# More places for turned blocks and queries, prepared weights stored by GpSimd, and right operands made early around the outer product with most sums

## The chip, the cores and the metric

The kernel runs on one core of a Trainium2 chip. The time is device microseconds of one execution, and the median of several executions is compared. Profiles show TensorE as PE (its weight loads as PEld), VectorE as DVE, ScalarE as ACT, GpSimd as POOL and the queue of SyncE, which issues most DMAs, as SP.

## The reference

A decoder layer in float32 on x of 16 x 128 x 1024, with three residual steps: self-attention with one head of 256, a linear cross-attention, and a gated feed-forward network whose weights are packed int4 with scale and zero for each group of 64.

```python
x = x + attn(layernorm(x), Wqkv, bqkv, Wo, bo)
x = x + xattn(layernorm(x), ctx, ctx, Wq, Wk, Wv, Wo, bo, g)
x = x + ffn(layernorm(x), gate, up, down)

def xattn(q, k, v, ...):          # channel-first, 8 heads of 64, n = 1024
    qh = softmax(Wq q, over the 64 of a head) * SCALE
    kh = softmax(Wk k, over n)
    context = einsum('bhdn,bhen->bhde', kh, Wv v)
    out = Wo einsum('bhde,bhdn->bhen', context, qh) + bo
    return out / max(norm(out), 1e-12) * g * sqrt(128)

def ffn(x, ...):                  # hidden 1024, inter 2752
    g, u = x @ Wg.T, x @ Wu.T     # Wg, Wu, Wd dequantized from int4
    return (silu(g) * u) @ Wd.T
```

## The kernel before

The order of work on each engine is that in which the Python code emits it; a tile framework adds the waits. Tiles come from pools with a fixed number of places (bufs): a new tile waits until the last reader of the tile that held its place is done. DMAs are issued in order by the queue of the engine that is named (SP, ACT or POOL), and several are in flight at once.

*Self-attention, 0 to 250 us.* Its last products, give_half, are emitted in the next stage: each of 8 calls multiplies half of a batch's attention output by Wo, and VectorE adds it to X and takes the batch's statistics. The two tiles of Wo are loaded again for them (wo_again, in the pool of the queries).

*Linear cross-attention, 250 to 855 us.* It goes over 16 batches (batches 8 to 15, then 0 to 7; k counts them). Each batch has eight ticks of some 3.9 us: key_unit and query_unit in turn, four times. Work is put off with later(n, fn), which runs fn at the n-th next tick. A query unit multiplies (kq) and ScalarE exponentiates (qe). Two ticks later weigh lets VectorE sum (sums) and invert (qrec) and POOL multiply qe. Four ticks later turn lets VectorE transpose 32 x 32 blocks into kt (pool b_kt), which a DMA on SP writes to DRAM as kd; one tick later four DMAs on SP read it as qs (pool b_qs), the turned queries. Keys go through ek, and VectorE sums them into ksum, whose column sums PE needs in mix for the small matrix m_sb of the batch. project_out multiplies qs by m_sb at the ticks in when, takes norms (on PE and ScalarE), and then VectorE scales (y), adds to X (add) and takes statistics; turned normalises the rows and turn_rows transposes them into kt as well, to be stored and loaded as the blocks of the feed-forward network (block_loads, 8 loads of 512 KB for each half of the batches). raise_flag tests all sums for overflow; count multiplies the result by ones on PE and VectorE copies the flag.

*Preparation beside it.* prepare is a generator, one step of which dequantizes half a 256-wide block of a weight matrix (DVE pa<-raw, pa<-pa,sz), or combines its quarters for Strassen's algorithm (pc), and stores all seven operands to DRAM, to wg, wu, wm, wr or wd. It runs in three parts: early (in the self-attention, stores on POOL), middle (in the cross-attention, two or three steps a batch, stores on SP) and rest (the down weights, in the feed-forward stage, stores on SP). prep_pools gives its pools: a places for pa, ahead + 1 for the loaded raw and sz.

*Feed-forward, 855 to 1774 us, and down projection, 1774 to 2254 us.* Two passes over 1024 rows each. Pass 0 takes blocks 0 to 3 with one level of Strassen (one_block; PE p<-b,w), then three pairs of blocks with two levels (two_levels, 1000 to 1274 us), then a last block; pass 1 takes five pairs with two levels. two_levels goes over outer products in the order DOWN = (1, 2, 6, 5, 3, 7, 4) for each pair; each has seven inner products p of eight matmuls (1.72 us). The right operands of outer q that are differences come from inner_right: four VectorE subtractions ti (k = 7, 5, 6, 4; p = 7, 5, 6, 4 read them). The left ones, li, come from POOL. The list right holds the steps for the next outer's ti, extra holds less urgent ones; do_extra(n, more) runs n of the first and more of the second between products. got adds finished products into the sums U, V and C on VectorE: 3 additions where q is 1, 11 where q is 7, and 7 for each other q. Then ScalarE takes SiLU of half of C and VectorE multiplies (h). PSUM is banked in turn between two pools of four.

The names that the change touches: pools b_kt and b_qs (lines 610 and 614), the middle preparation (620), count (691), block_loads (856), the ticks of give_half (941), when (954), prep_pools for the rest (1050), bufs of ti (1328) and the list right in two_levels (1497).

Of the kernel before, what the change touches and what calls it, by code (L numbers as in the profile page):

```python
# [11 lines left out]
F32 = mybir.dt.float32  # L12
# [6 lines left out]
P = 128  # L19
# [47 lines left out]
def decoder_layer(  # L67
# [482 lines left out]
    blocks = {}  # L550
    TOKENS = TB // Q

    def block_loads(p, blocks):

        for n, half in ((0, 0), (1, 0), (1, 1), (0, 1)):
            for i in range(2):
                src = xt_all[p][ds(half * BPT + 2 * i, 2), :, :, :, n]
                tc.keep_in_program_order(
                    nc.sync.dma_start(
                        blocks[n, half][:, ts(i, TOKENS // 2)],  # L560
                        src.rearrange("b a c i j t -> (c i) (b a) j t"),
                    )
                )
                yield
# [42 lines left out]
    b0 = unit_pool("b_0", 2)  # L607
    bw = unit_pool("b_w", 1)
    b3 = unit_pool("b_3", 3)
    bkt = side_pool("b_kt", 2)  # L610
    bpk = unit_pool("b_k", 2, space=PSUM)
    bs = side_pool("b_s", 1)
    bct = side_pool("b_ct", 2)
    bqs = side_pool("b_qs", 4)
    b1 = side_pool("b_1", 1)
    b2 = side_pool("b_2", 2)
    bps = side_pool("b_ps", 3, space=PSUM)

    prep_pools(sides, "x", 2, 1)
    middle = prepare(todo[EARLY:MIDDLE], 1, sync, vector, sync)  # L620


    pend = deque()
# [1 line left out]
    def later(n, fn):  # L625
        pend.append([n, fn])
# [10 lines left out]
    if True:  # L637
# [33 lines left out]
            sums = bs.tile([P, B * 4 * 2 * HEADS + B * 4], F32, name="sums")  # L671

        def sums_tile(n, at, name):
            return sums[:, ds(at, n)] if plain else small.tile([P, n], F32, name=name)

        def raise_flag():

            within = [small.tile([P, 1], F32, name=f"within{n}") for n in range(2)]
            for w, op, limit, test in zip(
                within, (ALU.max, ALU.min), (LIMIT, 1 / LIMIT), (ALU.is_le, ALU.is_ge)  # L680
            ):
                vector.tensor_reduce(w, sums, AX.X, op)
                vector.tensor_scalar(w, w, limit, None, test)
            vector.tensor_tensor(within[0], within[0], within[1], ALU.mult)

            def count():
                ps = bps.tile([P, 1], F32, name="mm")
                tensor.matmul(ps, ones, within[0], start=True, stop=True)
                vector.tensor_copy(flag, ps[0:1])

            later(2, count)

        def mix_weights():

# [14 lines left out]
        def key_shift(c_sb):  # L709

            shift = bas.tile([P, 4, P], F32, name="kshift")
            for oc in range(4):
                ps = bpk.tile([P, 2, 512], F32, name="kq")
                for h in range(2):
                    tensor.matmul(
                        ps[:, h, :], wk_sb[:, ts(oc, P)], c_sb[:, ts(h, 512)], start=True, stop=True
                    )
                nmax = small.tile([P, 1], F32, name="knmax")
                vector.tensor_reduce(nmax, ps, AX.XY, ALU.max, negate=True)
                vector.tensor_copy(shift[:, oc], nmax.to_broadcast([P, P]))  # L720
            return shift
# [45 lines left out]
        def mix(st):  # L767

            D = DIM_HEAD
            ks = bps.tile([P, 4], F32, name="mm")  # L770
            for r in range(4):
                tensor.matmul(
                    ks[:, r : r + 1], st["sum"][:, 0, ts(r, P)], ones[:, 0:1], start=True, stop=True
                )
            ksum = sums_tile(4, B * 8 * HEADS + 4 * st["b"], "ksum")
            krec = small.tile([P, 4], F32, name="krec")
            vector.tensor_copy(ksum, ks)
            vector.reciprocal(krec, ksum)
            kc = st["kc"]
            mp = bps.tile([P, 4, S], F32, name="mm")  # L780
            for r in range(4):

                for e in range(2):
                    tensor.matmul(
                        mp[ts(e, D), r, :],
                        kc[:, ds(r * P + e * D, D)],
                        g_sb[:, 2 * r + e, :],
                        start=True,
                        stop=True,
                    )  # L790
            st["m"] = b2.tile([P, 4, S], F32, name="m_sb")
            vector.tensor_tensor(
                st["m"], mp, krec.unsqueeze(2).to_broadcast([P, 4, S]), ALU.mult
            )

        def query_unit(b, pair, qs, wait):

            wide = [P, 2 * HEADS, DIM_HEAD]
            ps = bpk.tile([P, 2, 512], F32, name="kq")
            for i in range(2):  # L800
                tensor.matmul(
                    ps[:, i, :], xns[b][:, ts(2 * pair + i, P)], wq_sb, start=True, stop=True
                )
            heads = ps.rearrange("p i (h d) -> p (i h) d", d=DIM_HEAD)
            qe = b3.tile(wide, F32, name="qe")
            if plain:
                nc.scalar.activation(qe, heads, AF.Exp)  # L807
            else:
                mx = small.tile([P, 2 * HEADS], F32, name="qmx")
                vector.tensor_reduce(mx, heads, AX.X, ALU.max)  # L810
                vector.tensor_tensor(qe, heads, mx.unsqueeze(2).to_broadcast(wide), ALU.subtract)
                nc.scalar.activation(qe, qe, AF.Exp)

            def weigh():
                den = sums_tile(2 * HEADS, (4 * b + pair) * 2 * HEADS, "qden")
                rec = small.tile([P, 2 * HEADS], F32, name="qrec")
                vector.tensor_reduce(den, qe, AX.X, ALU.add)
                vector.reciprocal(rec, den)
                nc.gpsimd.tensor_tensor(qe, qe, rec.unsqueeze(2).to_broadcast(wide), ALU.mult)  # L819

            def turn():
                kt = bkt.tile([P, 4, NB, Q], F32, name="kt")
                vector.transpose(
                    kt.rearrange("p c n j -> p n c j"),
                    qe.rearrange("p h d -> p (h d)").rearrange("p (n c j) -> p n c j", c=4, j=Q),
                )
                kd = dram.tile([4, Q, 4, NB, Q], F32, name="kd", tag="kd", bufs=3)
                sync.dma_start(kd.rearrange("a i c n j -> (a i) c n j"), kt)  # L830

                def load():
                    qt = qs[pair] = bqs.tile([P, 4, NB, Q], F32, name="qs", tag="qs")
                    for c in range(4):
                        sync.dma_start(
                            qt[ts(c, Q)], kd[:, :, c].rearrange("a i n j -> i a n j")
                        )

                later(1, load)

            later(2, weigh)
            later(wait, turn)

        def turned(b):

            xn = b1.tile([P, 2 * JC, P], F32, name="xn3")
            for n in range(2):

                rows = X[b].rearrange("p (g j e n) -> p n j g e", g=16, j=JC, n=2)[:, n]
                dst = xn[:, ts(n, JC)].rearrange("p j (g e) -> p j g e", g=16)  # L850
                normalise_act(dst, rows, b)
            nc.gpsimd.dma_start(x_all[b], X[b])
            later(2, lambda: turn_rows(b, xn, bkt))
            if b == B - 1:
                blocks.update(new_blocks(xlate, lambda k: f"X{HB + 2 * k}"))
                loads = block_loads(0, blocks)
                for n in range(8):
                    later(7 + 2 * n, lambda: next(loads))

# [78 lines left out]

        for n in range(2 * BPT):
            later(  # L940
                n + 1,
                lambda n=n: give_half(B - BPT + n // 2, n % 2, oT, wo_again, bps, tensor, vector),
            )
        keys = {b: {"b": b} for b in batches}
# [3 lines left out]
        for k, b in enumerate(batches):  # L948
# [2 lines left out]


            if len(ahead) == 2:
                when = (13, 14, 15, 16, 17, 1, 1)
            elif ahead:
                when = (12, 13, 14, 15, 16, 1, 0)
            else:
                when = (10, 10, 11, 11, 12, 1, 0)
# [75 lines left out]
    with ExitStack() as gs:  # L1034
# [9 lines left out]
        def attention_done():  # L1044
# [2 lines left out]
            for _ in middle:  # L1047
                pass
            sides.close()
            prep_pools(second, "f", 3, 2)  # L1050
            rest = prepare(todo[MIDDLE:], 2, nc.sync, vector)
            banks.append(pool("c_u", 4, space=PSUM, side="right"))

# [248 lines left out]
        class Operands:  # L1302
# [5 lines left out]
            def inner_right(self, q):  # L1308
# [10 lines left out]
                def comb(k):  # L1319
                    if k == 7:  # L1320
# [4 lines left out]
                            F32,  # L1325
                            name="ti",
                            tag=tag,
                            bufs=1 if self.kept else 2,
                        )
                    dst = R[q, k] = R[q][:, (5, 6, 7, 4).index(k)]  # L1330
                    a, b = {
# [31 lines left out]
        def two_levels(ps, pairs, operands, between=lambda q: None):  # L1363
# [115 lines left out]
            for n, (i, q) in enumerate(OUTERS):  # L1479
# [13 lines left out]
                    soon_due.popleft()()  # L1493
                if q not in (1, 5):
                    sums["C"] = place.tile(wide, F32, name="C")
                if not last:
                    right.extend(operands.inner_right(OUTERS[n + 1][1]))
                if ps == 1 and n == 0:
                    extra.append(lambda: outer_operand(operands.T, 4))
                elif ps == 1 and n == 4:  # L1500
# [403 lines left out]
```

## Time and profile before

| what | us |
|---|---|
| median of 3 runs | 2255.17 (2254.84 to 2259.01) |
| the profiled execution | 2256.0, its span 2254.2 |
| PE busy | 2201.5 (98%) |
| VectorE busy | 1611.7 (71%) |
| ScalarE busy | 512.0 (23%) |
| GpSimd busy | 594.9 (26%) |
| mean granted clock of PE | 0.989 |

Shares of the whole span hide the stages: VectorE is busy for 92 us of every 100 between 300 and 600 us and for 58 to 86 of 100 from 600 to 1300 us. A list of waits is read as: engine, operation and line that waited, what ended the wait, total us, times, longest us. Most lines are 63, a helper that records operations, so groups are told apart by tiles: kt<-qe is the transposition of qe into kt. In a row of the stage table each engine has its busy us and in brackets its instructions, in the order PE, PEld, DVE, ACT, POOL; then follow the granted clock, the DMA share and GB/s.

### The profile page before, as it was taken

To read this page: it belongs to the slowest core of one execution; us is meant where nothing else is said; L and a number is where in the kernel's file an instruction comes from. 1 tells how busy PE (TensorE), PEld (TensorE's weight loads), DVE (VectorE), ACT (ScalarE), POOL (GpSimd) and SP (SyncE) were. 2 spreads that over 40 slices of the span, in tenths; PEclk is the share of its full clock that TensorE was granted. 3 is DMA by queue.
4 is the path that set the end of the run, shared out by engine and by line. 5 is a ranking of instruction groups with operands and counts; after the bars stand their busy time and mean duration, and the time that the engine had idled before them with its cause. 6 is when DMAs were issued, how large, how long until landed. Compare 5 with 4: busy or idle time off the path is not lost.

```text
span 2254.2 us, 24858 instructions
## 1 busy us (share of the span) xinstructions
PE 2201.5 (98%) x8666; PEld 1588.1 (70%) x8666; DVE 1611.7 (71%) x2185; ACT 512.0 (23%) x690; POOL 594.9 (26%) x450
## 2 busy tenths in 40 slices
PE   8999999999989999999999999999999999999998
PEld 7556555555545554458878678888887688888887
DVE  6997589999988656658888768787786545544462
ACT  2111135655545541111112111211211000000000
POOL 5452123333333320014434144444442000000000
PEclk9999999999999999999999999999999999999999
DMA  6445358888888569984333534554554974333731
GB/s 250 156 135 181 112 171 253 261 252 273 247 255 270 187 198 284 313 280 139 130 99 128 168 125 140 178 196 150 178 193 162 336 237 150 125 124 128 225 117 39
DMA packets 270006, 425.28 MB, mean 189 GB/s; under 512 B 28784, under 2 KB 130544, under 8 KB 269744
## 3 DMA queue, kind: packets, MB, share of 16 engines
q1 hardware_dynamic: 242752, 374.31, 52.4%
q0 software_dynamic: 9104, 30.68, 3.7%
q10 hardware_dynamic: 18016, 18.62, 2.6%
q8 instruction: 71, 1.16, 0.2%
q14 instruction: 63, 0.52, 0.1%
HBM read 265.62 MB, written 157.35 MB: 188 GB/s over the span
## 4 chain that ended last, share of the span: by engine, by line
PE 76%; DVE 14%; DMA 3%; issue 3%; POOL 2%; ACT 1%; SPq 0%; DVEq 0%; POOLq 0%; ACTq 0%
PE q L63 26%; PE po L1783 21%; PE p L63 10%; PE kq L63 4%; PE mm L63 4%; PE mm L397 4%; DVE pa L63 3%; PE kx L63 2%; PE mm L412 2%; DVE kt L63 2%; PE p L1160 2%; DVE sums L63 1%; PE mm L295 1%; DVE ti L63 1%; DVE pc L63 1%
## 5 line engine op out<-in xcount | busy, mean ns | idle before, releaser
L63 PE MATMUL q<-ti,li 128*128 128x256 f32 x1344 | 315.4, 384 | 11.0 <-DVE ti L63 10.2
L63 PEld LDWEIGHTS q<-ti,li 128*128 128x128 f32 x1344 | 257.6, 192 | 49.8 <-issue 9.9
L63 POOL TENSOR_TENSOR li<-w 128x512 f32<-128x512 f32 x112 | 159.9, 1429 | 258.2 <-DMA raw<-in_dq 140.6
L63 ACT COPY k<-q 128x512 f32<-128x512 f32 x168 | 98.4, 585 | 540.1 <-PE q L63 540.1
L819 POOL TENSOR_TENSOR qe<-qe,qrec 128x1024 f32<-128x1024 f32 x64 | 145.3, 2270 | 249.8 <-DVE qrec L63 206.3
L1783 PE MATMUL po<-wc,lc 128*128 128x256 f32 x840 | 183.4, 379 | 0.0
L1783 PEld LDWEIGHTS po<-wc,lc 128*128 128x128 f32 x840 | 159.6, 190 | 21.8
L63 PEld LDWEIGHTS mm<-qs,m_sb 128*128 128x128 f32 x512 | 99.0, 194 | 53.2 <-issue 38.0
L63 PE MATMUL mm<-qs,m_sb 128*128 128x256 f32 x512 | 124.9, 388 | 10.9 <-DMA qs<-kd 10.9
L63 PE MATMUL p<-b,w 128*128 128x512 f32 x304 | 133.9, 592 | 0.0
L63 POOL TENSOR_TENSOR li<-w,li 128x512 f32<-128x512 f32 x56 | 75.5, 1347 | 209.3 <-PE q L63 207.1
L1783 PE MATMUL po<-wq,lq 128*128 128x256 f32 x560 | 126.7, 379 | 0.4 <-issue 0.4
L63 PE MATMUL kx<-ek,cxt 128*128 128x512 f32 x256 | 125.6, 614 | 0.3 <-ACT ek L739 0.3
L63 PE MATMUL kq<-wq_sb,xn 128*128 128x512 f32 x256 | 121.7, 598 | 1.6 <-ACT qe L807 1.6
L63 PE MATMUL kq<-wk_sb,cx 128*128 128x512 f32 x256 | 122.0, 599 | 0.0
L63 PE MATMUL q<-b,w 128*128 128x256 f32 x512 | 120.9, 379 | 0.0
L63 DVE TENSOR_TENSOR C<-q,k 128x512 f32<-128x512 f32 x120 | 82.2, 685 | 53.4 <-PE q L63 51.2
L1783 PEld LDWEIGHTS po<-wq,lq 128*128 128x128 f32 x560 | 106.0, 190 | 16.0 <-issue 1.2
L63 DVE STREAM_TRANSPOSE kt<-qe 128x1024 f32<-128x1024 f32 x64 | 79.4, 1240 | 51.1 <-POOL qe L819 41.4
L397 PE MATMUL mm<-xnT,wqkv_sb 128*128 128x512 f32 (+1 forms) x320 | 113.1, 509 | 0.0
L63 DVE TENSOR_TENSOR pa<-pa,sz 128x1024 f32<-128x1024 int32 x86 | 108.8, 1265 | 3.6 <-DMA sz<-in_gsz 1.2
L63 PEld LDWEIGHTS p<-b,w 128*128 128x128 f32 x304 | 57.8, 190 | 71.9 <-issue 69.8
(196 smaller groups left out, 3844.0 us busy)
## 6 DMA issues: line engine op xcount, KB each, us to landing
lq<-h SPq DMA_DIRECT2D x140, 256.0 KB, 4.3
w<-wu SPq DMA_DIRECT2D x139, 256.0 KB, 3.2
w<-wg SPq DMA_DIRECT2D x133, 256.0 KB, 2.7
kd<-kt SPq DMA_DIRECT2D x64, 512.0 KB, 3.9
qs<-kd SPq DMA_DIRECT2D x256, 128.0 KB, 3.3
h<-hc SPq DMA_DIRECT2D x80, 256.0 KB, 2.8
wq<-wd SPq DMA_DIRECT2D x70, 256.0 KB, 5.3
h<-h SPq DMA_DIRECT2D x60, 256.0 KB, 2.1
```

Of the source, the lines that this page charges most:

```text
L63: return lambda *args, **kw: self._tc.keep_in_program_order(fn(*args, **kw))
L295: tensor.matmul(ps, oT[:, d, ts(b % BPT, S)], wo_d[d][:, ts(h, 512)], start=(d == 0), stop=(d == 1),)
L397: nc.tensor.matmul(ps[:, tokens], wqkv_sb[:, f, c, :], xnT[:, c, tokens], start=(c == 0), stop=(c == CC - 1),)
L412: nc.tensor.matmul(ps, xnT[:, c, ts(i, S)], wqkv_sb[:, 4:6, c, :], start=(c == 0), stop=(c == CC - 1),)
L819: nc.gpsimd.tensor_tensor(qe, qe, rec.unsqueeze(2).to_broadcast(wide), ALU.mult)
L1160: tensor.matmul(ps, wt[:, j, :], T[q][:, :, j], start=(first == q and j == 0), stop=(q in (2, 3, 4) and j == JC - 1), skip_group_check=True,)
L1783: nc.tensor.matmul(bank[:, i, :], l[:, ts(i, S)], w,  start=(start and c == 0 and i % 2 == 0), stop=(stop and c == len(pairs) - 1), skip_g ...
```

## The change

Ten edits. The pools of turned blocks and of queries get a place more each (2 to 3, 4 to 5), and small tiles of the cross-attention a pool of their own. The middle preparation stores by POOL's queue instead of SP's. The blocks of pass 0 are loaded by ScalarE's queue. The flag is counted four ticks after it is raised instead of two. The eight give_half calls start two ticks later. project_out begins one tick later in all but the last batches. The rest of the preparation has two places for pa instead of three. The ti have three places in pass 0 instead of two; there the operands for q = 4 are no longer made during q = 7 but put into extra during q = 3, beside those for q = 7.

```diff
--- before.py
+++ after.py
@@ -550,13 +550,13 @@
     blocks = {}
     TOKENS = TB // Q
 
-    def block_loads(p, blocks):
+    def block_loads(p, blocks, queue=nc.sync):
 
         for n, half in ((0, 0), (1, 0), (1, 1), (0, 1)):
             for i in range(2):
                 src = xt_all[p][ds(half * BPT + 2 * i, 2), :, :, :, n]
                 tc.keep_in_program_order(
-                    nc.sync.dma_start(
+                    queue.dma_start(
                         blocks[n, half][:, ts(i, TOKENS // 2)],
                         src.rearrange("b a c i j t -> (c i) (b a) j t"),
                     )
@@ -607,17 +607,18 @@
     b0 = unit_pool("b_0", 2)
     bw = unit_pool("b_w", 1)
     b3 = unit_pool("b_3", 3)
-    bkt = side_pool("b_kt", 2)
+    bkt = side_pool("b_kt", 3)
     bpk = unit_pool("b_k", 2, space=PSUM)
     bs = side_pool("b_s", 1)
     bct = side_pool("b_ct", 2)
-    bqs = side_pool("b_qs", 4)
+    bqs = side_pool("b_qs", 5)
+    bsm = side_pool("b_sm", 4)
     b1 = side_pool("b_1", 1)
     b2 = side_pool("b_2", 2)
     bps = side_pool("b_ps", 3, space=PSUM)
 
     prep_pools(sides, "x", 2, 1)
-    middle = prepare(todo[EARLY:MIDDLE], 1, sync, vector, sync)
+    middle = prepare(todo[EARLY:MIDDLE], 1, nc.gpsimd, vector, sync)
 
 
     pend = deque()
@@ -671,11 +672,11 @@
             sums = bs.tile([P, B * 4 * 2 * HEADS + B * 4], F32, name="sums")
 
         def sums_tile(n, at, name):
-            return sums[:, ds(at, n)] if plain else small.tile([P, n], F32, name=name)
+            return sums[:, ds(at, n)] if plain else bsm.tile([P, n], F32, name=name)
 
         def raise_flag():
 
-            within = [small.tile([P, 1], F32, name=f"within{n}") for n in range(2)]
+            within = [bsm.tile([P, 1], F32, name=f"within{n}") for n in range(2)]
             for w, op, limit, test in zip(
                 within, (ALU.max, ALU.min), (LIMIT, 1 / LIMIT), (ALU.is_le, ALU.is_ge)
             ):
@@ -688,7 +689,7 @@
                 tensor.matmul(ps, ones, within[0], start=True, stop=True)
                 vector.tensor_copy(flag, ps[0:1])
 
-            later(2, count)
+            later(4, count)
 
         def mix_weights():
 
@@ -715,7 +716,7 @@
                     tensor.matmul(
                         ps[:, h, :], wk_sb[:, ts(oc, P)], c_sb[:, ts(h, 512)], start=True, stop=True
                     )
-                nmax = small.tile([P, 1], F32, name="knmax")
+                nmax = bsm.tile([P, 1], F32, name="knmax")
                 vector.tensor_reduce(nmax, ps, AX.XY, ALU.max, negate=True)
                 vector.tensor_copy(shift[:, oc], nmax.to_broadcast([P, P]))
             return shift
@@ -773,7 +774,7 @@
                     ks[:, r : r + 1], st["sum"][:, 0, ts(r, P)], ones[:, 0:1], start=True, stop=True
                 )
             ksum = sums_tile(4, B * 8 * HEADS + 4 * st["b"], "ksum")
-            krec = small.tile([P, 4], F32, name="krec")
+            krec = bsm.tile([P, 4], F32, name="krec")
             vector.tensor_copy(ksum, ks)
             vector.reciprocal(krec, ksum)
             kc = st["kc"]
@@ -806,14 +807,14 @@
             if plain:
                 nc.scalar.activation(qe, heads, AF.Exp)
             else:
-                mx = small.tile([P, 2 * HEADS], F32, name="qmx")
+                mx = bsm.tile([P, 2 * HEADS], F32, name="qmx")
                 vector.tensor_reduce(mx, heads, AX.X, ALU.max)
                 vector.tensor_tensor(qe, heads, mx.unsqueeze(2).to_broadcast(wide), ALU.subtract)
                 nc.scalar.activation(qe, qe, AF.Exp)
 
             def weigh():
                 den = sums_tile(2 * HEADS, (4 * b + pair) * 2 * HEADS, "qden")
-                rec = small.tile([P, 2 * HEADS], F32, name="qrec")
+                rec = bsm.tile([P, 2 * HEADS], F32, name="qrec")
                 vector.tensor_reduce(den, qe, AX.X, ALU.add)
                 vector.reciprocal(rec, den)
                 nc.gpsimd.tensor_tensor(qe, qe, rec.unsqueeze(2).to_broadcast(wide), ALU.mult)
@@ -853,7 +854,7 @@
             later(2, lambda: turn_rows(b, xn, bkt))
             if b == B - 1:
                 blocks.update(new_blocks(xlate, lambda k: f"X{HB + 2 * k}"))
-                loads = block_loads(0, blocks)
+                loads = block_loads(0, blocks, nc.scalar)
                 for n in range(8):
                     later(7 + 2 * n, lambda: next(loads))
 
@@ -938,7 +939,7 @@
 
         for n in range(2 * BPT):
             later(
-                n + 1,
+                n + 3,
                 lambda n=n: give_half(B - BPT + n // 2, n % 2, oT, wo_again, bps, tensor, vector),
             )
         keys = {b: {"b": b} for b in batches}
@@ -951,7 +952,7 @@
 
 
             if len(ahead) == 2:
-                when = (13, 14, 15, 16, 17, 1, 1)
+                when = (14, 15, 16, 17, 18, 1, 1) if k < 13 else (13, 14, 15, 16, 17, 1, 1)
             elif ahead:
                 when = (12, 13, 14, 15, 16, 1, 0)
             else:
@@ -1047,7 +1048,7 @@
             for _ in middle:
                 pass
             sides.close()
-            prep_pools(second, "f", 3, 2)
+            prep_pools(second, "f", 2, 2)
             rest = prepare(todo[MIDDLE:], 2, nc.sync, vector)
             banks.append(pool("c_u", 4, space=PSUM, side="right"))
 
@@ -1325,7 +1326,7 @@
                             F32,
                             name="ti",
                             tag=tag,
-                            bufs=1 if self.kept else 2,
+                            bufs=1 if self.kept else 3,
                         )
                     dst = R[q, k] = R[q][:, (5, 6, 7, 4).index(k)]
                     a, b = {
@@ -1493,8 +1494,11 @@
                     soon_due.popleft()()
                 if q not in (1, 5):
                     sums["C"] = place.tile(wide, F32, name="C")
-                if not last:
+
+                if not last and not (ps == 0 and q == 7):
                     right.extend(operands.inner_right(OUTERS[n + 1][1]))
+                if ps == 0 and q == 3:
+                    extra.extend(operands.inner_right(OUTERS[n + 2][1]))
                 if ps == 1 and n == 0:
                     extra.append(lambda: outer_operand(operands.T, 4))
                 elif ps == 1 and n == 4:
```

## The prediction, made before the changed kernel was run

> **What bounds the kernel now.** I read the busy line first, then TensorE's waits, then the table by stage, then VectorE's waits in the stage with most stalls. From the page, and from the list of what ended each idle time of PE:
>
> ```profile
> PE 2201.5 (98%) x8666; PEld 1588.1 (70%) x8666; DVE 1611.7 (71%) x2185; ACT 512.0 (23%) x690; POOL 594.9 (26%) x450
> ```
>
> ```profile
> PE mm L63 <- DMA qs<-kd: 10.9, 4, 6.3
> PE q L63 <- DVE ti L63: 10.6, 8, 3.3
> PE tr L344 <- ACT xn L152: 9.2, 1, 9.2
> PE mm L63 <- DMA wo_again<-in_wo: 4.9, 2, 3.4
> PE mm L63 <- DVE within L63: 2.9, 1, 2.9
> PE kq L63 <- ACT qe L807: 1.6, 1, 1.6
> PE mm L63 <- DVE ksum L63: 1.6, 2, 1.1
> ```
>
> PE bounds it: 98% busy, and no product is taken away. Its waits (total us, times, longest) sum to 44.7 us, 9.2 of them at the very start, which nothing here touches. The stage table adds a second loss (after the three figures of each engine: granted clock, DMA share, GB/s):
>
> ```profile
> 200.00:300.00 100.00, 95.05 (x290) 50.59 (x288) 60.32 (x103) 16.13 (x26) 18.19 (x29) 0.97 0.43 142
> 300.00:400.00 100.00, 98.90 (x342) 54.78 (x342) 91.97 (x116) 49.66 (x56) 33.30 (x18) 0.98 0.76 234
> ...
> 500.00:600.00 100.00, 97.59 (x328) 54.36 (x327) 92.28 (x117) 56.34 (x66) 36.43 (x19) 0.98 0.81 256
> 600.00:700.00 100.00, 91.83 (x299) 50.54 (x298) 79.44 (x104) 49.83 (x58) 31.02 (x17) 0.95 0.88 269
> ...
> 1000.00:1100.00 100.00, 95.98 (x431) 83.36 (x430) 79.22 (x95) 18.59 (x29) 42.90 (x30) 0.97 0.42 134
> 1100.00:1200.00 100.00, 96.13 (x430) 83.25 (x429) 85.60 (x103) 18.50 (x29) 43.10 (x31) 0.97 0.39 130
> 1200.00:1300.00 100.00, 97.21 (x380) 72.80 (x379) 77.97 (x97) 17.06 (x27) 27.30 (x20) 0.98 0.51 154
> ```
>
> Where PE stalls, its clock drops below 1: the records show 3.41 or 6.83 us at half speed behind each longer gap, which is a product of 379 ns taking 767. One minus the clock, times 100 us, is what each row loses: 3, 2, 2, 5, 3, 3, 2, and 2 more in 800 to 900, 22 us in all. So all that can be won is 44.7 - 9.2 + 22 = 57.5 us, 2.5%, in three places: the start of the linear attention (255 us), its middle with its end (to 855 us), and the two-level products (1000 to 1274 us).
>
> VectorE in the middle, 300 to 680 us:
>
> ```profile
> DVE kt L63 <- POOL qe L819: 20.0, 11, 2.1
> DVE kt L63 <- DMA kd<-kt: 3.8, 2, 3.2
> DVE pa L63 <- DMA raw<-in_gq: 2.9, 1, 2.9
> DVE shift L63 <- POOL rstd L136: 2.3, 6, 0.4
> DVE pa L63 <- DMA sz<-in_gsz: 1.2, 1, 1.2
> DVE ksum L63 <- PE mm L63: 0.3, 1, 0.3
> ```
>
> These 30.5 us and 92% busy of 380 us (350) fill the stage: VectorE practically never waits for PE or ScalarE. It sets the pace there, and its lag comes out as PE's stalls on turned queries.
>
> **The change part by part.** The sum is made against the profiled execution: 2256.0 us, span 2254.2, 0.8 above the median.
>
> *Start.* The products of the first half's end (give_half) start two ticks later, and their two loads of Wo come ahead of two context loads in SP's order. Before, the first was issued at 250.3 us and PE waited at 255.4 (3.40) and 258.1 (1.55). In the new order SP's last wait ahead of it is for a PE product that ended at 244.7 us; with the 5 us of landing seen here it should be in by 250. Gain: 4.95 of gap and 3 of clock, 8.0. The eight additions and statistics behind those products also move two ticks (some 8 us) into VectorE's full stage; that counts in the middle. Bounds: 5 (one gap stays) to 8.4.
>
> *End of the attention.* The flag's product waits two ticks more, 2 x 1.72 us of products in front of it against a wait of 2.9: gone, with the 2 us of clock of that row. Gain 4.9 (bounds 2 to 5). What waits for it, the release of the attention's pools and the next preparation, starts 3.4 us later; in 850 to 1000 us PE is 150.0 of 150.0 busy, so that is covered.
>
> *Middle, the gain.* A third place for turned blocks and a fifth for queries remove VectorE's two waits for kd (3.8). The 72 stores of prepared weights leave SP for POOL: SP issues in order, and with about eight transfers outstanding it waits for landings. Queries turned at 651 us were stored at 655.0 and their load landed at 670.3, 19 us, against 11.7 for the same chain at 418 us. This late SP explains the 6.3 us gap and the 4.1 us of raw and sz. Project_out also starts a tick (3.9 us) later, so every query load has that much more room. PE's stalls there are 10.9 + 1.6, with 9 of clock: 21.5.
>
> *Middle, the price.* On POOL 72 stores by 0.56 us (its own rows wg<-pc, 561 ns) are 40 us over 435, where it is a third busy; each can delay a qe by up to 0.56, and VectorE waits for qe anyway (11 waits). Moving project_out changes VectorE's order. The y scaling (1.17 us) had filled its wait for qe and no longer does (+0.35 a batch). An operation with two SBUF operands that meets a qe on POOL ends only with it (ksum 2.10 us instead of 1.18, pc 2.38 instead of 0.69): one such meeting more for ksum (+0.85), one for the X addition (about +0.2); shift no longer waits for rstd (-0.4). Net +1.0 us a batch (bounds +0.4 to +1.5), over 11 batches +11 (4 to 16). The late X additions cost some 3 us of lag at 293 us (0 to 5). Against that, 7.9 us of VectorE's DMA waits go, and the lag that the late SP added to the query chain, some 8 us. So +14 - 16 = -2 us, between a full gain of 21.5 and, if SP's part stays and the price is at its upper end, +13. I take -2: VectorE remains the limit, and its next late result is ksum, whose margin before PE's product was already 0.05 us in two batches.
>
> The Trainium skill ("Advanced Engine Details and Errata", VectorE Performance Modes) says that VectorE's second SBUF port is shared with GpSimd and that they block each other. It speaks against giving POOL more work; yet pc beside POOL's DMA issues took 685 ns against 684 without, so this trace shows no such price for stores, only for qe. By the rule applied to all 72 stores, at 0.56 us each, the sum would be 40 us of VectorE worse; I keep the row.
>
> *Block loads on ACT.* Eight loads of 512 KB leave SP for ScalarE's queue. What they wait for landed 10 us before ScalarE comes to them, so each costs its issue, 0.4 to 1.3 us, on an engine 50 to 57% busy. ScalarE also changes its order of functions: 43 table loads of 1.28 us instead of 36. PE waited for ScalarE's qe once, 1.6. I take +1 (0 to 4).
>
> *Two places instead of three for the down weights' pa (855 to 1277 us).* VectorE must see the stores of two units back landed. Stores land about 5 us after issue there, DMA share 0.98 to 1.04; with three places the longest such wait was 5.9 us (892 us), without PE stalling. From one matrix's second pa to the next matrix's first there were 6 to 18 us. VectorE is 66% busy with 51 us idle in 150. I take +1 (0 to 8).
>
> *Right operands made early.* In each pair the products of q=4 waited for ti (3.29 at 1079.8, 3.28 at 1172.0, 2.21 at 1263.1): 8.8, with 8 of clock. q=7 has most sums, 11 additions, and the 4 operands of q=4 besides. These 4 now go between those of q=7, one outer earlier: q=7 falls from 17 operations to 13, q=3 rises from 13 to 17. Walked through by hand from the second pair's rows: q=7's third operand was ready at 1154.98 and needed at 1156.50; two more subtractions of 0.69, stretched by a POOL li of 1.27 that starts at 1155.09, make it about 1156.9. So 0.4 us are lost there, and the later sums leave 0 to 0.6 at the next pair's first outer: 0.6 a pair, 1.8 in all. Gain 15 (bounds 8, if the new gaps are 1.5 us and one in two drops the clock, to 16.8). The small waits before q=3 (0.2 and 0.4) stay.
>
> Sum: -8.0 - 4.9 - 2 + 1 + 1 - 15 = -28, so 2228.
>
> On the clock the Trainium skill ("TensorE: Matmul & The Clock Gate", Part 1) says that the clock halves only after an idle window of about 3.4 us. The rows differ: a gap of 1.10 us at 319.9 was followed by 3.41 us at half speed, one of 1.64 at 780 by none. By the rule as stated, only gaps such as 6.3 and 3.4 would pay, and the two-level gain would be nearer 9 than 15.
>
> **The rivals.**
> *The middle is won as well (15%).* For it: the three longest query waits follow late SP issues. Against it: VectorE's 92%. All of 21.5 instead of 2: 2208.
> *VectorE gives it all back (20%).* The waits move from qs to ksum and qe, and the middle is 11 worse than before instead of 2 better. For it: ksum's 0.05 us of margin. Against: the tick of room. 2228 + 13 = 2241.
> *Slower, by the pa places (11%).* If each of the 16 later units waits 5.9 us as the one at 892 did, VectorE needs 94 us and has 51 idle: 43 come out on PE, 2256 - 29 + 43 = 2270. It turns the sign from 80 us of waiting, that is 14 such units. For it: DMA share 1. Against: 6 to 18 us of distance for 5 us of landing.
> *No change (6%).* The early operands make q=7 as late as q=4 was (-15 falls away) and the middle is 11 worse: near 2256.
>
> **How the numbers follow.** The forecast has 48%. Its own range, from the bounds: 2216 to 2242. The range of 8 in 10 takes in the first two rivals: 2206 to 2258. Some 4.5 us (0.2%) is what a measurement of this kernel can tell from no change. Faster: forecast, first and second rival, 83%; same 6%; slower 11%.
>
> **What would show it.** Right: no PE wait for wo_again or within; ti waits under 3 us in all, the clock 1.00 in 1000 to 1270; VectorE still at 92% in 300 to 600 us with PE waiting for ksum or qs, some 10 to 20 us with the clock's part; no kd wait on VectorE. Wrong: PE at 99% in 300 to 700 us (first rival), VectorE's waits for wd stores above 50 us with PE gaps in 860 to 1000 us (third), PE waits for ti at q=7 above 2 us a pair (fourth).

## The result and the profile after

The changed kernel takes 2263.27 us (median of 8 runs, 2260.81 to 2266.81) against 2255.36 us in the same sessions: 1.0039 times the time before, interval 1.0021 to 1.0056. It is slower by 8 us where 27 less were forecast. The profiled execution is the slowest of the eight, 2266.8 us with a span of 2265.0, so the two profiled executions lie 10.8 us apart.

The busy line of the page, then PE's waits (engine, operation, line, what ended the wait, total us, times, longest):

```profile
PE 2197.5 (97%) x8666; PEld 1584.4 (70%) x8666; DVE 1634.5 (72%) x2185; ACT 519.9 (23%) x697; POOL 634.9 (28%) x522
```

```profile
PE mm L63 <- DMA qs<-kd: 18.0, 5, 6.4
PE p L1161 <- DVE h L63: 11.2, 1, 11.2
PE tr L344 <- ACT xn L152: 9.2, 1, 9.2
PE kx L63 <- ACT ek L740: 7.3, 3, 4.8
PE mm L63 <- DVE ksum L63: 2.7, 3, 1.5
PE q L63 <- ACT k L63: 2.6, 4, 0.7
PE q L63 <- DVE ti L63: 1.8, 5, 0.6
```

The waits for wo_again and for the flag (within) are gone, and those for ti fell from 10.6 to 1.8 us. In their place stand a wait for h of 11.2 us that did not exist, one for ek of 7.3, and the waits for turned queries rose from 10.9 to 18.0. The stage table (after the engines' busy us: clock, DMA share, GB/s):

```profile
200.00:300.00 100.00, 100.00 (x324) 53.97 (x323) 66.67 (x113) 19.98 (x29) 20.32 (x33) 1.00 0.46 154
300.00:400.00 100.00, 93.25 (x309) 51.11 (x308) 92.06 (x113) 49.24 (x55) 44.80 (x36) 0.97 0.79 246
...
500.00:600.00 100.00, 96.53 (x326) 53.49 (x325) 92.25 (x113) 60.22 (x69) 43.86 (x37) 0.98 0.78 251
600.00:700.00 100.00, 84.02 (x269) 46.72 (x268) 79.04 (x97) 45.87 (x53) 35.89 (x28) 0.91 0.77 233
...
800.00:900.00 100.00, 88.31 (x230) 43.92 (x229) 42.20 (x60) 33.80 (x44) 8.56 (x10) 0.95 0.67 189
...
1000.00:1100.00 100.00, 97.37 (x400) 75.07 (x399) 80.54 (x97) 16.04 (x27) 39.48 (x28) 1.00 0.60 185
1100.00:1200.00 100.00, 98.52 (x451) 84.91 (x450) 88.98 (x109) 19.39 (x30) 46.74 (x33) 1.00 0.39 130
1200.00:1300.00 100.00, 98.69 (x414) 77.99 (x414) 85.37 (x105) 18.97 (x29) 34.77 (x24) 1.00 0.47 141
```

The two-level products run at full clock now, as forecast, and so does the start at 200 to 300 us. What was lost lies at 300 to 400, at 600 to 700 (84 us busy, clock 0.91) and at 800 to 900 us. VectorE's waits at 300 to 680 us:

```profile
DVE kt L63 <- POOL qe L820: 16.6, 8, 2.1
DVE pa L63 <- DMA raw<-in_gq: 11.2, 1, 11.2
DVE kt L63 <- DMA xt<-kt: 4.2, 2, 2.1
DVE kt L63 <- DMA kd<-kt: 3.8, 2, 3.2
DVE pa L63 <- DMA sz<-in_gsz: 0.4, 1, 0.4
```

The busy share of VectorE is 92% up to 600 us, as before; but a raw load came 11.2 us late, although 72 stores had left SP's queue, and the kd waits were not less. SP was held by something new.

To place gains and losses, the profiled executions are cut at PE's first query product of batch k (k = 2, 3, 10, 13 in the order of work), at the first product of the feed-forward network (F), the first two-level product (G), the end of the first two-level stage (H) and the end of pass 1's two-level products (I). Lengths in us; the last column is the median of the runs of each session.

| kernel | to k=2 | to 3 | to 10 | to 13 | to F | to G | to H | to I | median |
|---|---|---|---|---|---|---|---|---|---|
| before | 346.1 | 31.5 | 226.5 | 107.7 | 73.7 | 214.0 | 274.1 | 462.7 | 2255.4 |
| after | 334.1 | 39.2 | 226.7 | 122.1 | 75.5 | 224.1 | 262.1 | 462.7 | 2263.3 |
| block loads on SP | 334.8 | 37.7 | 229.6 | 99.5 | 80.9 | 225.4 | 262.1 | 462.7 | 2252.6 |
| two kt places | 333.7 | 31.2 | 234.4 | 115.9 | 80.4 | 217.5 | 262.1 | 462.8 | 2255.8 |
| old ticks | 335.5 | 31.5 | 231.2 | 109.9 | 76.1 | 226.0 | 262.1 | 462.7 | 2255.3 |
| loads on SP, two places | 334.1 | 31.2 | 234.4 | 101.1 | 81.1 | 216.5 | 262.1 | 462.7 | 2245.6 |
| all three undone | 335.9 | 31.5 | 227.8 | 109.1 | 73.6 | 215.4 | 262.1 | 462.8 | 2236.4 |
| before + early ti | 345.3 | 31.5 | 226.3 | 107.9 | 73.7 | 216.6 | 262.4 | 462.7 | 2246.3 |
| before + third kt place | 339.0 | 31.5 | 228.5 | 106.8 | 76.1 | 223.8 | 274.2 | 462.9 | 2261.5 |

From before to after: -12.0 at the start, +7.7, +0.2, +14.4 and +1.8 in the middle, +10.1 at the end of the attention, -12.0 in the two-level products, 0.6 more behind: +10.8 in all, the difference of the two profiled executions. So three losses have to be explained: batch 2 to 3, batch 10 to 13, and F to G.

### The profile page after: what moved, and what is told of

It is laid out like the page before. It is cut to its first block, busy times and chain, and to the rows that moved or that the text cites. A ratio compares the mean times of both kernels' runs of the same rounds, so it can differ in the third digit from the quotient of the medians.

```text
span 2265.0 us, 24956 instructions
## 1 busy us (share of the span) xinstructions
PE 2197.5 (97%) x8666; PEld 1584.4 (70%) x8666; DVE 1634.5 (72%) x2185; ACT 519.9 (23%) x697; POOL 634.9 (28%) x522
## 3 DMA queue, kind: packets, MB, share of 16 engines
q8 instruction: 71, 1.16, 0.2%
## 4 chain that ended last, share of the span: by engine, by line
PE 72%; DVE 16%; DMA 5%; issue 4%; POOL 1%; ACT 1%; SPq 1%; DVEq 0%; POOLq 0%; ACTq 0%
PE q L63 26%; PE po L1787 21%; PE p L63 8%; PE mm L397 4%; DVE pa L63 4%; PE mm L63 3%; PE kq L63 3%; PE p L1161 2%; DVE kt L63 2%; PE mm L412 2%; DVE sums L63 2%; DVE ti L63 2%; PE kx L63 2%; DVE ksum L63 1%; PE mm L295 1%
## 5 line engine op out<-in xcount | busy, mean ns | idle before, releaser
L820 POOL TENSOR_TENSOR qe<-qe,qrec 128x1024 f32<-128x1024 f32 x64 | 152.9, 2390 | 135.8 <-DVE qrec L63 112.9
```

## The experiments

**One part undone, or one done alone.** Four kernels, the first two from the changed kernel, the others from the kernel before.

```diff
-                loads = block_loads(0, blocks, nc.scalar)
+                loads = block_loads(0, blocks)
```

> The changed kernel with one part undone: the eight block loads go by SP's queue again. Theory A (shared bookkeeping of transfers: SP holds back its own turned-query loads until a block load that ScalarE issues late has landed): SP's waits for b<-xt (37.0 us, 6 times) go, PE's waits for qs between 600 and 720 us fall from 18.0 us to 8 or less, and with their half-clock stretches the time falls by 10 to 20 us, to about 2248. Theory B (VectorE's own lag makes the query waits): the waits keep their sum within 4 us and the time stays at 2263 within 4.

Measured: 2252.57 us, 1.0002 times the kernel before (0.9990 to 1.0015): 10.7 us better than the changed kernel. SP's waits, 600 to 720 us, in the changed kernel:

```profile
SPq L63 <- DMA b<-xt: 43.4, 7, 8.4
SPq L63 <- DMA kd<-kt: 25.3, 6, 6.5
```

and with the block loads on SP:

```profile
SPq L63 <- DMA kd<-kt: 38.7, 10, 5.9
SPq L63 <- DVE kt L63: 8.5, 4, 4.3
```

In the changed kernel SP stood for 43 us until block loads had landed that ScalarE had issued. In its timeline of SP's queue the next transfers come at once when such a load is in:

```profile
624.29 0.55 SPq L63 DMA_DIRECT2D raw<-in_gq  x1
633.27 0.40 SPq L63 DMA_DIRECT2D sz<-in_gsz  x1
```

Between them SP did nothing for 8.4 us: a load that ScalarE issued at 627.49 landed at 633.25. PE's waits for turned queries, with the block loads on SP:

```profile
PE mm L63 <- DMA qs<-kd: 2.2, 1, 2.2
```

They fell from 18.0 to 2.2 us and the stretch from batch 10 to 13 from 122.1 to 99.5 us, 8 less than before the change. Theory A holds: the two queues were coupled, and moving a transfer to another engine's queue made SP wait for that engine's pace. Why the compiled program couples them (a shared set of completion counters would do it) was not tried apart.

```diff
-    bkt = side_pool("b_kt", 3)
+    bkt = side_pool("b_kt", 2)
```

> The changed kernel with one part undone: two places for turned blocks instead of three. The built order on the engines then has the context loads behind the first Wo load again, the last products with turned queries ten products earlier, and the row normalisations behind y and sq on ScalarE. Theory A (these moves of order are what the third place does): PE's 4.9 us wait for wo_again returns with 3 us of clock (+8), the 11.2 us gap at 870 shrinks to under 4 (-8 or more, and 3 to 5 of clock), the ScalarE ek waits of 7.3 us fall under 3 (-4 and 3 of clock): about 2252. Theory B (the third place only keeps VectorE from waiting): VectorE's waits for kd grow by some 4 us, the 11.2 us gap stays: about 2270.

Measured: 2255.80 us, 1.0009 (0.9996 to 1.0021), 7.5 better than the changed kernel. The gap near 860 us fell to 3.5 us and the ek waits to 4.0. So theory A holds for the end of the attention. The wait for wo_again did not return, against my expectation: the later give_half alone is enough to avoid it.

```diff
-                            bufs=1 if self.kept else 2,
+                            bufs=1 if self.kept else 3,
...
-                if not last:
+                if not last and not (ps == 0 and q == 7):
                     right.extend(operands.inner_right(OUTERS[n + 1][1]))
+                if ps == 0 and q == 3:
+                    extra.extend(operands.inner_right(OUTERS[n + 2][1]))
...
-            prep_pools(second, "f", 3, 2)
+            prep_pools(second, "f", 2, 2)
```

> The kernel before with one part of the change: right operands for q=4 made during q=3, three places for ti, and (there is no space otherwise) two places for pa in the rest of the preparation. Theory A: the 8.8 us of ti waits and 8 us of half clock between 1000 and 1274 us go, nothing comes back: 2243 to 2247 (-8 to -12 by what the changed kernel shows in that stage). Theory B (two places for pa slow the stage ahead of it): PE gaps or a lower clock in 855 to 1000 us, the time within 4 of 2255.

Measured: 2246.26 us, 0.9972 (0.9961 to 0.9982): 7.9 us faster. The two-level stage takes 262.4 instead of 274.1 us. The stretch ahead of it, with two places for pa, takes 216.6 instead of 214.0, with a PE wait for sg of 1.1 us that was not there; the rest is clock, as the flag's wait of 2.9 us is followed by 6.83 us at half speed there and by 3.41 before. The places cost little.

The kernel before with three places for turned blocks and nothing else:

> The kernel before with one part of the change: three places for turned blocks instead of two. Theory A (order): the wo_again wait at 255 us goes (-8), the last products with turned queries come ten products later and PE stalls behind VectorE's late sums near 860 us as in the changed kernel (+8 to +12): 2253 to 2260. Theory B (only VectorE's waits for kd go): -4 to -12 and no gap near 860.

Measured: 2261.53 us, 1.0040 (1.0025 to 1.0054). One more place makes the kernel slower by as much as the whole change does. Its start is 7 us shorter (the wo_again waits fall from 4.9 to 1.6), and its end from F to G is 9.8 longer, with a gap of 10.6 us at 855. The flag is still counted early there, so it is the flag's product that waits:

```profile
PE mm L63 <- DVE within L63: 10.6, 1, 10.6
```

Theory A holds, 1.5 us beyond its range. The number of places alone changed the order of PE's instructions: with three, 94 matmuls of the feed-forward network stand ahead of the last products with turned queries, with two 74. So the order on an engine isn't simply that in which the Python code emits it, as I had put it at the start; how the framework settles it was not studied.

**Do the gains add?** All from the changed kernel: block loads on SP and two kt places, then with the old ticks as well, then the first again with the stores on SP; and the kernel before with early ti, later give_half and later flag.

> The changed kernel with two parts undone: two places for turned blocks, block loads by SP's queue. If the two losses found (ScalarE's block loads, 10.7 us by one run; the third place's late last products, 7.5 by the other) are separate, the gains add: 2263.3 - 10.7 - 7.5 = 2245. If both only freed the same lag of VectorE, they don't add: 2252 or more. PE's gap near 860 us should stay under 4 us and SP should not wait for b<-xt in either case.

Measured: 2245.62 us, 0.9963 (0.9948 to 0.9977). They add: 2245 was expected.

```diff
-                when = (14, 15, 16, 17, 18, 1, 1) if k < 13 else (13, 14, 15, 16, 17, 1, 1)
+                when = (13, 14, 15, 16, 17, 1, 1)
```

> As the run before it, and project_out at its old ticks. Theory A (the later tick spoils ScalarE's order: 42 table loads instead of 36, and PE waits for ek, sq and ksum by 13.6 us in the run without the third place): these waits fall to about 4 us, and the time is 4 to 8 us below the run before it. Theory B (the tick gives the queries room): PE's qs waits grow by 5 us or more and the time is 3 to 8 us above.

Measured: 2236.44 us, 0.9923 (0.9894 to 0.9952): 9.2 us better by the medians, 5.1 by the two profiled spans. PE's waits with the later tick, in the run before this one (without it: ksum 1.5, qs 13.8, and no line for sq or ek):

```profile
PE mm L63 <- DVE ksum L63: 7.8, 8, 1.7
PE mm L63 <- DMA qs<-kd: 5.6, 4, 2.5
PE p L1161 <- DMA w<-wg: 3.9, 1, 3.9
PE p L1161 <- DVE h L63: 3.5, 1, 3.5
PE q L63 <- ACT k L63: 3.2, 5, 0.7
PE mm L63 <- ACT sq L882: 2.6, 3, 1.1
PE kx L63 <- ACT ek L740: 2.2, 2, 1.4
```

Both theories were partly right. The tick gives the queries their room: qs waits of 5.6 instead of 13.8, and 8.0 us less from batch 10 to 13. But it takes 6.6 us from batch 3 to 10 through ksum, sq and ek, and 7.5 from batch 13 to F.

> As the first run of this set, and the middle preparation stores by SP's queue as in the kernel before. Theory A (72 stores on GpSimd make its qe products late and with them VectorE's ksum): PE's ksum waits fall from some 7 us to 2 and the time by 2 to 5 us. Theory B (SP is the queue that is short of time): raw, sz and kd waits on VectorE and qs waits on PE near 670 us grow, the time by 3 to 8 us.

Measured: 2249.53 us, 0.9986 (0.9973 to 1.0000), 3.9 above the same kernel with the stores on GpSimd. PE's ksum waits did fall, from 7.8 to 3.5 us, but qe and sq waits on ScalarE rose by more. VectorE's waits for kd stayed (7.8 and 7.4) and PE's for queries fell from 5.6 to 4.1, so the time went as theory B has it, but hardly by the waits that it named; the cause stays open.

> The kernel before with three parts: the early right operands (with two places for pa), give_half two ticks later, the flag counted two ticks later. Theory A: against the run with the early operands alone (2246) the wo_again wait (4 us and 2 of clock) and the flag's (2.9 and 3) go: 2236 to 2240. Theory B (VectorE's lag in the middle grows by the moved additions): 2244 to 2248, with PE's ksum or qs waits up by 5 us or more between 300 and 700 us.

Measured: 2240.57 us, 0.9941 (0.9921 to 0.9961): 5.7 below the early ti alone. Neither wait is there any more. But where PE waited for the flag before, it now waits for the first block's h, 0.6 us longer. First the early ti alone, then this kernel:

```profile
PE mm L63 <- DVE within L63: 2.9, 1, 2.9
```

```profile
PE p L1161 <- DVE h L63: 3.5, 1, 3.5
```

From F to G it takes 216.2 us instead of 216.6: the later flag gains next to nothing, and what this kernel gains is the start, 339.1 instead of 345.3 us up to batch 2. Queries cost 13.6 us instead of 11.2.

**Each remaining part by itself.** The first undoes one part of the changed kernel; the other three change one part of the fastest kernel so far.

> The changed kernel with one part undone: project_out at its old ticks. If the later tick costs the same by itself as with two other parts undone (9.2 us between the two runs there), 2254; the 4.8 us ek wait at 357 us and its half-clock stretch go, as xn, y and sq come to ScalarE in another order; the 18 us of qs waits and the 11.2 us gap near 870 us stay. If the tick gave the queries room, the qs waits grow and the time stays within 4 of 2263.

Measured: 2255.26 us, 1.0004 (0.9995 to 1.0013), 8.0 better than the changed kernel. The 11.2 us wait for h stays, as expected; the query waits did not stay, but fell from 18.0 to 11.2 us, although SP still waits 28.1 us for block loads between 600 and 720 us. The ek wait at 357 us goes, and with it 7.7 us from batch 2 to 3. It needs both the third place and the later tick: it is gone in each kernel that lacks one of them. In the changed kernel ScalarE has a row normalisation ahead of ek, which waits for a shift that VectorE computes late:

```profile
ACT xn L152 <- DVE shift L63: 10.4, 1, 10.4
```

> The changed kernel with the block loads on SP and project_out at its old ticks, and the third place for turned blocks kept. Against the same kernel with two places (2236.4) it shows the third place alone: an 11 us gap near 850 us instead of 3.5, and a longer half-clock stretch, so 2246 (+8 to +12); if what is left to win in the middle by a third place (VectorE's kd waits of 6.6 us there) outweighs it, 2232 to 2238.

Measured: 2250.91 us, 0.9985 (0.9974 to 0.9996), 14.5 above the same kernel with two kt places (8 to 12 were expected), by the profiled executions 14: 2.5 from batch 13 to F and 11.5 from F to G, at most 1 either way elsewhere. VectorE's waits for kd did fall, from 6.6 us to 0.4; PE's time to batch 13 is the same all the same.

> As the fastest run so far (two places for turned blocks, block loads on SP, old ticks), and four places for queries instead of five. If the fifth place matters, PE's or SP's waits on the query loads grow and the time rises by 2 to 5 us, to 2239 or more. If it never bound, 2236 within 2.

Measured: 2239.61 us, 0.9931 (0.9916 to 0.9946).

> As the fastest run so far, and the middle preparation stores by SP's queue. If SP is short of time, the raw and kd waits on VectorE rise from 6.6 us to 12 and the time by 3 to 5 us, to 2240. If 72 stores on GpSimd cost as much by late qe products as they save SP, 2236 within 2.

Measured: 2235.89 us, 0.9920 (0.9901 to 0.9939). The intervals of both overlap that of the fastest kernel. The fifth query place may be worth some 3 us, though PE's query waits did not grow without it (12.7 against 13.8). With the stores on SP VectorE's raw and kd waits rose from 6.6 to 11.8 us, as expected if SP is short of time, but the time did not. The runs don't settle either part, and with the later tick the queue had looked like 4 us.

**The last batch's end.** What the third place costs at the end was put down to VectorE's order: h behind y. With three places (and the other two parts undone) the last batch's y was moved, and with it its addition to X and its statistics, which follow at the same number of ticks:

```diff
-                when = (10, 10, 11, 11, 12, 1, 0)
+                when = (10, 10, 11, 11, 12, 4, 0)
```

> The kernel with three places for turned blocks, block loads on SP and old ticks (2250.9), and the last batch's scaling y three ticks later, so that VectorE multiplies the first block's h ahead of it instead of waiting 23.5 us for ScalarE's sq. If the third place's price at the end is that h stands behind y, PE's 11.2 us gap falls under 4 us, its half-clock stretch from 13.65 to 6.8 us or less, and the time by 8 to 14 us, to about 2240. If the gap has another cause (weights that land late, the products' own order), it stays above 8 us and the time within 3 of 2251.

Measured: 2242.18 us, 0.9941 (0.9920 to 0.9963), 8.7 below the same kernel with y early. The 11.2 us gap and the 13.65 us at half speed around it are gone, and from F to G the kernel takes 208.9 us instead of 226.9: the order of h behind y and what follows it was the cause. VectorE's wait at the end in the changed kernel, 830 to 880 us:

```profile
DVE y L63 <- ACT sq L891: 23.5, 1, 23.5
```

and with y late, 840 to 880 us:

```profile
DVE y L63 <- ACT sq L891: 3.1, 1, 3.1
```

Of the 18 us 7 are given back in the two-level products of pass 1, where PE has a new gap of 3.6 us at 1306 with 6.8 us at half speed, for which the profile shows no releaser.

> The same with two places for turned blocks (2236.4): the last batch's y two ticks later, past the first block's h. PE's gap is 3.5 us there with 3.4 us at half speed, so at most 5 us can go: 2231 to 2236 if nothing comes back. If the later end of the attention delays the rest of the preparation, VectorE's waits for down weights and PE's for h grow after 860 us, and the time is 2236 to 2242.

Measured (two ticks later instead of three): 2234.63 us, 0.9905 (0.9881 to 0.9929), the fastest kernel of all by its median, but its interval overlaps those of the same kernel with y early (2236.44) and of that with the stores on SP (2235.89). From F to G it is 6 us shorter than with y early, as PE's wait for h falls from 3.5 to 0.4 us, and pass 1 is 5 us longer.

## Why the prediction was wrong

*Start (forecast -8.0).* Right in size: 346.1 to 334.1 us up to batch 2, part of which is only work that moved behind that mark; PE is 100% busy at 200 to 300 us. Done with the early ti and the later flag, the later give_half takes 6.2 us off the stretch up to batch 2 and leaves no wait for wo_again; the third kt place by itself leaves 1.6 of 4.9 us.

*End of the attention (forecast -4.9).* Wrong, and one of three steps that failed. I costed two ticks of slack for the flag and took the order of the last products for granted. The flag's wait did go, but the first block's h, which frees PE's banks, stands behind the last batch's y on VectorE as the flag's test does, and PE then waits for h. With two places that wait is 3.5 us where the flag's was 2.9, so that the gain of 4.9 was not there to be had: 0.4 measured. The third place, which I had priced only as a gain (VectorE's 3.8 us of kd waits), moved the products of the last batch 20 matmuls later. ScalarE's sq and VectorE's y followed, and h with them: 11.2 us. Instead of -4.9 the stretch from F to G took +10.1. One place alone does it (before + third place), and moving y and its steps takes it away. Undone in the changed kernel, the third place gives 7.5 us back by the medians, and 14.5 where the other two parts are undone.

*Block loads on ACT (forecast +1, bounds 0 to 4).* Wrong, and the second. I priced their issue on ScalarE and looked at what they wait for; I didn't ask who waits for them. SP did, for 43 us. Measured: 10.7 us by the medians.

The Trainium skill ("DMA: Bandwidth & Descriptors", Issuing engines are not separate DMA queues) says that transfers started on different engines share the same 16 DMA engines, and that spreading them saves only the issue time. This trace goes further: there was less than nothing to save, since SP's queue waited for ScalarE's transfers.

*Middle (forecast -2, bounds -21.5 and +13).* Wrong in sign, and the third: +24 from batch 2 to F. Part of it is SP's waits for block loads. The 7.9 us of VectorE's DMA waits that were to go became 19.6 (300 to 680 us); with the block loads on SP raw, sz and kd waits are gone. Beside it stands the later tick, whose price I set against a larger gain. That it costs order on VectorE and ScalarE while it gives the queries room was right: 6.6 and 7.5 us lost, 8.0 won where two other parts are out of the way, and 5.1 lost in all between the two profiled executions (9.2 by the medians). In the changed kernel the tick costs 8.0, and there even the query waits are longer with it. Not foreseen: the ek wait of 4.8 us, with 6.83 us at half speed around it, that tick and third place make together.

*Down weights' pa (forecast +1).* Near: the stretch ahead of the two-level products took 2.6 more, of which 1.1 is a wait.

*Early right operands (forecast -15, bounds -8 to -16.8).* Right in kind, 12.0 us in the stage and 7.9 in the median when done alone. The stage's rows, before and after (from G to H):

```profile
999.43:1273.53 274.10, 263.42 (x1177) 228.15 (x1176) 227.44 (x273) 49.52 (x77) 113.30 (x80) 0.97 0.39 126
```

```profile
1021.69:1283.79 262.10, 258.06 (x1178) 222.03 (x1177) 228.64 (x276) 49.12 (x77) 114.83 (x80) 1.00 0.42 137
```

PE idles 4.0 us instead of 10.7: 6.6 less, close to the 8.8 less 1.8 for new gaps in the sum. The new gaps are waits for ScalarE's k (four of 0.6 to 0.7 us, where there was one). The term of the sum that was too large is the 8 us of clock: no half-speed record is left, yet PE is busy only 5.4 us less. What took the other 2.6 us stands in no wait on the list; that short waits for k do it is likely and not shown.

*The rivals.* None of them named what happened. The one that ends slower had the sign right by luck: it was hung on the places of pa, which cost 2.6 us; the real mechanisms were three parts that I had put near nothing or at a gain. Without the block loads, the third place and the tick the other terms gain some 17 us (2236.4 against 2253.3 in the same sessions) of the 27 that they sum to: the early operands and the start most of theirs, the flag nothing. Nor was the range the sum of its parts: with every term at its upper bound the sum is 2266.

On the clock the Trainium skill ("TensorE: Matmul & The Clock Gate", Part 1) was right in the large here: 11.2 us idle brought 10.24 us at half speed, and gaps of 0.6 to 1.5 us between 569 and 610 us none. But in the same execution 2.5 us at 672.7 were enough for 3.41, and so were 1.16 us at 512.3.

## What to carry to other kernels

A place more in a pool is not free of risk where a framework orders the instructions: compare the built order of every engine, not only of the one that waited, down to the last use in the stage, and ask what stands behind each moved instruction. When a wait is to be taken away, ask which wait ends next at the same place. When a transfer moves to another engine's queue, look for who waits for its landing, on the old queue above all. Undo parts of a change one by one: here three of ten cost some 27 us and the others gained some 17.

## What was not expected of the hardware

How far one late result reaches through the clock. These are the rows of the stretch from F to G, with y early and with y late (three kt places, block loads on SP, old ticks):

```profile
780.69:1007.62 226.93, 213.44 (x514) 98.98 (x515) 125.21 (x174) 47.98 (x68) 16.47 (x16) 0.96 0.81 242
```

```profile
781.57:990.42 208.85, 208.35 (x514) 97.50 (x515) 122.11 (x168) 48.00 (x68) 16.90 (x16) 1.00 0.83 251
```

PE does the same 514 matmuls in both. It idles 13.5 us in the first and 0.5 in the second, and is busy 5.1 us longer in the first, at a clock of 0.96: of the 18.1 us, 13.0 are idle and 5.1 are clock. Moving one scaling and its steps behind four multiplications on VectorE gained both; pass 1 took 7 us of it back. Some 1.7 of the clock's part may be chance: both kernels have a gap of 2.4 us for weights at the start of the stretch, and only in the first do 3.41 us at half speed follow it, at 782.0.
